# Cutting the first eight output tiles into smaller stores, and a later place for the scale and shift of two row groups

## Chip, cores, metric

One core of one Trainium2 chip (the other cores idle). The metric is the device time of one execution in microseconds.

## The reference, cut

Batch norm (training statistics, over the batch and the 16 x 16 block) of the outer products of all pairs of feature rows, then a multiplication by one 16 x 16 weight:

```python
# r_xi, r_xj: (1024, 39, 16); the 741 pairs are those with col < row
cross = xj[:, rows, :, None] * xi[:, cols, None, :]
mean = jnp.mean(cross, axis=(0, 2, 3), keepdims=True)
var = jnp.mean(jnp.square(cross - mean), axis=(0, 2, 3), keepdims=True)
normed = (cross - mean) * jax.lax.rsqrt(var + BN_EPS)
normed = normed * gamma[None, :, None, None] + beta[None, :, None, None]
out = normed[:, :, None, :, :] * W[None, None, :, :, :]     # 1024 x 1 x 741 x 16 x 16, f32
```

The inputs are 5 MB, the output 777 MB. Whatever else the kernel does, it has to write 777 MB.

## The kernel before

The batch lies on 128 partitions, 8 samples each. The statistics come first (to 37 us). Then the output is made tile by tile: a tile is one feature row `r` with its `r` pairs, for two samples of every partition. The tiles go in the order 19 (four tiles), then 20 and 18, 21 and 17, and so on to 38, so that the two tiles of every such couple have 38 pairs together. `y_sb` has room for two couples, so for four tiles: tile 12 goes where tile 8 and the first columns of tile 9 were. (In the profile DVE is VectorE, ACT is ScalarE, POOL is GpSimd and PE is TensorE; SP is SyncE, which issues the stores.)

Tiles 0 and 1 are made as raw products while the statistics run, and scaled, shifted and weighted when these are there. From tile 2 on, `xi` is scaled ahead (`scale_xi`, POOL), ACT and POOL make the products, and DVE adds the shift and multiplies by the weight in one instruction per pair (`finish`).

```python
ONE, TWO = 24, 31
FIRST_PIECES = ((0, 2, 8, 19), (0, 9, 19))
POOL_I, POOL_I_LONG = 4, 5
POOL_SHARE = 0.13
...
def products(n):
    xs = xs_of.pop(n)
    split = E - (POOL_I_LONG if tiles[n][0] > TWO else POOL_I)
    for t in range(T):
        for i in range(E):
            product(n, nc.scalar if i < split else nc.gpsimd, t, i, xs[:, t])

def store(n, c0, c1):                       # pairs c0 to c1 of tile n
    ...
    step = 1 if r > ONE and c1 == r else T
    for t in range(0, T, step):
        nc.sync.dma_start(out_v[...], view(n)[:, t : t + step, c0:c1, :]...)

def weigh(n, bounds):                       # tiles 0 and 1: times the weight, then store
    for c0, c1 in zip(bounds, bounds[1:]):
        nc.vector.tensor_tensor(y[:, :, c0:c1, :], y[:, :, c0:c1, :], w_dve..., ALU.mult)
        store(n, c0, c1)

def bounds(r):
    pieces = 1 + (r > ONE) + (r > TWO)
    return tuple(q * r // pieces for q in range(pieces + 1))

def finish(n):                              # tiles 2 and up
    split = r - int(r * POOL_SHARE + 0.5)
    ...                                     # POOL does pairs split to r
    for c0, c1 in zip(bounds(r), bounds(r)[1:]):
        for c in range(c0, min(c1, split)):
            stt(y[:, :, c, :], y[:, :, c, :], t_sb[...], w_dve..., ALU.add, ALU.mult)   # DVE
        store(n, c0, c1)
...
apply(0)                  # scale and shift of row 19, from PSUM into st_sb (DVE)
affine(0)                 # tile 0: scale and shift, ACT and POOL in turn
weigh(0, FIRST_PIECES[0])
scale_xi(2)
apply(1)                  # rows 15 to 18
apply(2)                  # rows 20 to 24
affine(1)
weigh(1, FIRST_PIECES[1])
for n in range(1, len(tiles)):
    if n == 1:
        products(2)
        scale_xi(3)
        continue
    if n + 2 < len(tiles):
        scale_xi(n + 2)
    finish(n)
    ...                   # apply of the later groups behind tiles 8, 16 and 24
    if n + 1 < len(tiles):
        products(n + 1)
```

## Time and profile before

| | before |
|---|---|
| median (lowest to highest) | 1895.81 us (1895.78 to 1895.99), 3 runs |
| span of the profiled execution | 1894.1 us |
| written | 776.99 MB |
| busy: DVE, ACT, POOL | 91%, 86%, 83% |
| DMA from 80 to 1850 us | share 0.98 to 1.04 in every stretch of 10 us and more |

A line of a view by stretches has the stretch and its length in us, the busy time and (in brackets) the instructions of PE, its weight load PEld, DVE, ACT and POOL, the granted clock, the DMA share (the mean busy share of the 16 DMA engines) and GB/s. A hole is a time in which the DMA moves nothing because no store is ready.

The chain that ended last, followed back from the end, in a stretch of the middle (start, length, what):

```profile
1418.35 4.62 DVE y_sb L233 x7
...
1423.03 13.14 DMA out_dram<-y_sb
...
1436.28 3.69 ACT y_sb L137 x6
...
1441.72 4.62 DVE y_sb L233 x7
```

A store lands, ACT may fill the place that has come free, DVE weights the products, the next store is issued and waits its turn in a full queue. A store's way from issue to landing (13.14 us) is over half of such a round (23 us from one DVE line to the next), and the DMA is busy throughout the round (share 1.00 from 1400 to 1600 us). Second, the instructions of ACT in the order of time around the first waits for a landed store (start, length, engine, line, operation, and in brackets the idle time before with what ended it):

```profile
170.63 1.51 ACT L137 ACTIVATE y_sb<-xs,xj_sb 128x336 f32<-128x336 f32 x3 [5.18 <-DMA out_dram<-y_sb]
```

At 170.63 us ACT has waited 5.18 us for tile 9 to land, whose place it needs for the second sample of tile 12. This moment will serve as a clock: it says when the stream of stores has got through tile 9, about 130 us after the first store.

### The profile page before, as it was taken

Reading aid. Unit: us, or ns where it says so; the run is one execution under the profiler, and the core shown is the slowest. Engines: PE = TensorE matmul, PEld = TensorE weight load, DVE = VectorE, ACT = ScalarE, POOL = GpSimd, SP = SyncE. Lnnn points to the kernel's source line nnn. Section 1 sums busy time; section 2 is a strip of 40 time slices with the busy share of each in tenths; the row PEclk is TensorE's granted clock in tenths of the full one; section 3 lists DMA queues with packets and bytes.
Section 4 is the critical chain, followed back from the end, with each engine's and each line's share of the span. In section 5 each row is a group of like instructions: output and inputs, shape, how many; then the busy total and the mean of one; then the engine's idle time right before and its main releaser. Section 6 shows DMA issues by size and latency. Waiting matters only on the chain. (4 is left out here: it accounts for less than half of the span.)

```text
span 1894.1 us, 10252 instructions
## 1 busy us (share of the span) xinstructions
PE 24.5 (1%) x128; PEld 23.1 (1%) x128; DVE 1730.9 (91%) x2609; ACT 1621.5 (86%) x3625; POOL 1574.5 (83%) x1985
## 2 busy tenths in 40 slices
PE   3100000000000000000000000000000000000000
PEld 3100000000000000000000000000000000000000
DVE  7999999998989898989898989899999999999996
ACT  8998989898989897989898989888888888888762
POOL 9797878787878787878787878898888888888972
DMA  3899999999999999999999999999999999999999
GB/s 147 362 426 430 425 430 426 427 428 422 430 424 425 424 425 425 424 426 424 423 426 424 425 424 422 424 421 421 421 421 421 418 414 420 414 418 417 417 418 389
DMA packets 67567, 783.67 MB, mean 414 GB/s; under 512 B 4896, under 2 KB 6048, under 8 KB 13728
## 3 DMA queue, kind: packets, MB, share of 16 engines
q1 hardware_dynamic: 66912, 780.46, 97.9%
q10 hardware_dynamic: 576, 2.56, 0.3%
q14 instruction: 78, 0.64, 0.1%
q8 instruction: 1, 0.02, 0.0%
HBM read 6.00 MB, written 776.99 MB: 413 GB/s over the span
## 5 line engine op out<-in xcount | busy, mean ns | idle before, releaser
L233 DVE SCALAR_TENSOR_TENSOR y_sb<-y_sb,st_sb,w_dve 128x512 f32<-128x512 f32 x2542 | 1678.7, 742 | 134.9 <-issue 133.0
L137 ACT ACTIVATE y_sb<-xs,xj_sb 128x256 f32<-128x256 f32 (+32 forms) x3544 | 1576.5, 537 | 228.4 <-DMA out_dram<-y_sb 170.3
L139 POOL TENSOR_SCALAR y_sb<-xs,xj_sb 128x560 f32<-128x560 f32 (+35 forms) x1256 | 643.0, 534 | 39.4 <-DMA out_dram<-y_sb 31.1
L225 POOL TENSOR_TENSOR y_sb<-y_sb,w_sb 128x1024 f32<-128x1024 f32 (+4 forms) x138 | 441.9, 3202 | 11.5
L157 POOL TENSOR_TENSOR xs<-xi_sb,st_sb 128x576 f32<-128x576 f32 (+37 forms) x150 | 187.8, 1252 | 225.9 <-ACT y_sb L137 213.8
L221 POOL TENSOR_SCALAR y_sb<-y_sb,st_sb 128x512 f32<-128x512 f32 x384 | 259.4, 691 | 13.1 <-ACT y_sb L137 13.1
L202 DVE TENSOR_TENSOR y_sb<-y_sb,w_dve 128x1024 f32<-128x1024 f32 (+4 forms) x5 | 20.9, 4205 | 3.9 <-ACT y_sb L192 3.9
L137 ACT ACTIVATE y_sb<-xi_sb,xj_sb 128x304 f32<-128x304 f32 x40 | 18.7, 534 | 0.1
L409 PE MATMUL ps<-y_sb 39*128 39x38 f32 (+37 forms) x76 | 16.5, 397 | 5.5 <-DVE y_sb L397 5.5
L409 PEld LDWEIGHTS ps<-y_sb 39*128 39x128 f32 x76 | 16.3, 329 | 5.7 <-issue 5.7
L192 ACT ACTIVATE y_sb<-y_sb,st_sb 128x512 f32<-128x512 f32 x20 | 14.2, 798 | 0.0
L194 POOL TENSOR_SCALAR y_sb<-y_sb,st_sb 128x512 f32<-128x512 f32 x18 | 13.5, 766 | 0.3 <-issue 0.3
L139 POOL TENSOR_SCALAR y_sb<-xi_sb,xj_sb 128x304 f32<-128x304 f32 x24 | 11.9, 528 | 0.0
L294 DVE TENSOR_REDUCE y_sb<-y_sb 128x78 f32<-128x1248 f32 x8 | 11.1, 1443 | 0.0
L288 ACT ACTIVATE y_sb<-y_sb 128x1248 f32<-128x1248 f32 x8 | 9.9, 1244 | 1.3 <-POOL y_sb L278 1.3
L272 DVE TENSOR_REDUCE y_sb<-xj_sb 128x78 f32<-128x1248 f32 (+1 forms) x5 | 5.9, 1189 | 5.5 <-DMA xj_sb<-in_r_xj_dram 5.5
L278 POOL TENSOR_TENSOR y_sb<-xj_sb,y_sb 128x1248 f32<-128x1248 f32 x4 | 9.3, 2322 | 1.9 <-ACT y_sb L322 1.9
L278 POOL TENSOR_TENSOR y_sb<-xi_sb,y_sb 128x1248 f32<-128x1248 f32 x4 | 9.3, 2329 | 0.0
L311 PE MATMUL ps<-y_sb 128*39 128x79 f32 x48 | 7.2, 339 | 16.6 <-DVE y_sb L294 16.6
L311 PEld LDWEIGHTS ps<-y_sb 128*39 128x39 f32 x48 | 6.1, 183 | 17.5 <-DVE y_sb L294 9.6
L272 DVE TENSOR_REDUCE y_sb<-xi_sb 128x78 f32<-128x1248 f32 (+1 forms) x5 | 5.9, 1186 | 0.1
L254 POOL TENSOR_SCALAR_AFFINE_SELECT y_sb<-y_sb 39x4992 f32<-39x4992 f32 x1 | 4.6, 4624 | 0.0
(45 smaller groups left out, 16.9 us busy)
## 6 DMA issues: line engine op xcount, KB each, us to landing
out_dram<-y_sb SPq DMA_DIRECT2D x32, 3072.0 KB, 13.7
out_dram<-y_sb SPq DMA_DIRECT2D x29, 2816.0 KB, 15.5
out_dram<-y_sb SPq DMA_DIRECT2D x32, 1664.0 KB, 14.3
out_dram<-y_sb SPq DMA_DIRECT2D x16, 3328.0 KB, 17.1
out_dram<-y_sb SPq DMA_DIRECT2D x12, 3840.0 KB, 17.6
out_dram<-y_sb SPq DMA_DIRECT2D x29, 1536.0 KB, 15.4
out_dram<-y_sb SPq DMA_DIRECT2D x12, 3584.0 KB, 18.4
out_dram<-y_sb SPq DMA_DIRECT2D x20, 1792.0 KB, 17.7
```

The source lines that it names most:

```text
L137: nc.scalar.activation(y, src, AF.Copy, scale=scale)
L139: engine.tensor_scalar(y, src, scale, 1.0, ALU.mult, ALU.mult)
L157: nc.gpsimd.tensor_tensor(xs, xi_sb[:, t0 : t0 + T, 0:r, :], s_sb[:, :, n0 : n0 + r, :].to_broadcast([P, T, r, E]), ALU.mult,)
L192: nc.scalar.activation(y[:, :, c, :], y[:, :, c, :], AF.Identity, bias=t_c, scale=s_c)
L194: nc.gpsimd.tensor_scalar(y[:, :, c, :], y[:, :, c, :], s_c, t_c, ALU.mult, ALU.add)
L202: nc.vector.tensor_tensor(y[:, :, c0:c1, :], y[:, :, c0:c1, :], w_dve.unsqueeze(1).to_broadcast([P, T, c1 - c0, EE]), ALU.mult,)
L221: nc.gpsimd.tensor_scalar(y[:, :, c, :], y[:, :, c, :], t_sb[:, n0 + c : n0 + c + 1], 1.0, ALU.add, ALU.mult)
L225: nc.gpsimd.tensor_tensor(y[:, :, split:r, :], y[:, :, split:r, :], w_sb.unsqueeze(1).to_broadcast([P, T, r - split, EE]), ALU.mult,)
L233: stt(y[:, :, c, :], y[:, :, c, :], t_sb[:, n0 + c : n0 + c + 1], w_dve.to_broadcast([P, T, EE]), ALU.add, ALU.mult,)
L278: nc.gpsimd.tensor_tensor(devs[n % 7], sources[x][:, t0 : t0 + T], shift[:, x : x + 1, :].unsqueeze(3).to_broadcast([P, T, F, E]), ALU.sub ...
L311: nc.tensor.matmul(acc[0:F, 0 : 2 * F + 1], lhs, fb[:, t], start=t == 0, stop=t == NT - 1)
L409: nc.tensor.matmul(ps[:, :, first[r] - n0 : first[r] - n0 + r], pick[:, r, :], stq[:, :, 0:r], start=True, stop=True,)
```

## The change

Intent: let the stream of stores run without holes in its first 40 us, by sending pieces as soon as they are weighted, and keep scale and shift of two row groups, which nobody needs yet, from standing ahead of tile 1. The core of the diff:

```diff
-FIRST_PIECES = ((0, 2, 8, 19), (0, 9, 19))
+FIRST_PIECES = (
+    (0, 2, 5, 9, 14, 19), (0, 6, 12, 19), (0, 4, 11, 19), (0, 9, 19), (0, 10, 20), (0, 9, 18), (0, 10, 20), (0, 9, 18)
+)
 ...
-    def bounds(r):
+    def bounds(n):
+        if n < len(FIRST_PIECES):
+            return FIRST_PIECES[n]
+        r = tiles[n][0]
         pieces = 1 + (r > ONE) + (r > TWO)
 ...
-        weigh(0, FIRST_PIECES[0])
+        weigh(0)
         scale_xi(2)
+        affine(1)
+        weigh(1)
+        apply(2)
         apply(1)
-        apply(2)
-        affine(1)
-        weigh(1, FIRST_PIECES[1])
```

(`weigh` and `finish` now ask `bounds(n)` instead of being given the bounds.)

More of the change, by code (lines that the diff above doesn't have):

```diff
@@ L196, in affine, with weigh @@
                 )
-    def weigh(n, bounds):
+    def weigh(n):
         y = view(n)
-        for c0, c1 in zip(bounds, bounds[1:]):
+        for c0, c1 in zip(bounds(n), bounds(n)[1:]):
             nc.vector.tensor_tensor(
@@ L230, in finish @@
             )
-        for c0, c1 in zip(bounds(r), bounds(r)[1:]):
+        for c0, c1 in zip(bounds(n), bounds(n)[1:]):
             for c in range(c0, min(c1, split)):
```

## The prediction

> **What bounds the kernel now.** I read four views in this order: the page's head, busy time by stretches, the instructions in order of time from 37 to 180 us, and the chain that ended last. The page first:
>
> ```profile
> PE 24.5 (1%) x128; PEld 23.1 (1%) x128; DVE 1730.9 (91%) x2609; ACT 1621.5 (86%) x3625; POOL 1574.5 (83%) x1985
> DMA  3899999999999999999999999999999999999999
> GB/s 147 362 426 430 425 430 426 427 428 422 430 424 425 424 425 425 424 426 424 423 426 424 425 424 422 424 421 421 421 421 421 418 414 420 414 418 417 417 418 389
> ```
>
> No compute engine is full, but the output (777 MB written) leaves at 414 to 430 GB/s from the third slice to the last but one, with the DMA digit at 9. So the end is set by when the stream of stores begins, by its holes, and by its rate. Holes show only in the first two slices (47 us each). Busy time by stretches there:
>
> ```profile
> 42.00:72.00 30.00, 11.19 (x52) 10.98 (x52) 28.90 (x23) 30.00 (x60) 23.80 (x34) 1.00 0.80 332
> 72.00:76.00 4.00, 0.00 (x0) 0.00 (x0) 4.00 (x7) 4.00 (x10) 2.45 (x4) 1.00 0.00 0
> 76.00:146.00 70.00, 0.00 (x0) 0.00 (x0) 69.97 (x109) 70.00 (x160) 64.61 (x84) 1.00 1.00 427
> ```
>
> Last two columns: DMA share and GB/s. From 42 to 72 us a fifth of the DMA time is empty, from 72 to 76 us all of it, after 76 us none. DVE is full in all three, so in this stretch DVE is what the DMA waits for. The instructions in order of time (start, length, engine) say why:
>
> ```profile
> 39.10 14.19 ACT L192 ACTIVATE y_sb<-y_sb,st_sb 128x512 f32<-128x512 f32 x20
> 40.00 1.22 DVE L202 TENSOR_TENSOR y_sb<-y_sb,w_dve 128x1024 f32<-128x1024 f32 x1 [2.14 <-ACT y_sb L192]
> 42.12 3.35 DVE L202 TENSOR_TENSOR y_sb<-y_sb,w_dve 128x3072 f32<-128x3072 f32 x1 [0.89 <-ACT y_sb L192]
> 46.35 6.02 DVE L202 TENSOR_TENSOR y_sb<-y_sb,w_dve 128x5632 f32<-128x5632 f32 x1 [0.88 <-ACT y_sb L192]
> ...
> 53.20 105.48 ACT L137 ACTIVATE y_sb<-xs,xj_sb 128x304 f32<-128x304 f32 x240
> ...
> 53.62 10.34 DVE L202 TENSOR_TENSOR y_sb<-y_sb,w_dve 128x4608 f32<-128x4608 f32 x2
> ...
> 63.94 77.11 DVE L233 SCALAR_TENSOR_TENSOR y_sb<-y_sb,st_sb,w_dve 128x512 f32<-128x512 f32 x117
> ...
> 159.75 5.70 ACT L137 ACTIVATE y_sb<-xs,xj_sb 128x336 f32<-128x336 f32 x12 [1.07 <-DMA out_dram<-y_sb]
> ```
>
> A store leaves only when its whole piece is weighted. A "pair" (one column of a tile, two rows of the batch) is 256 KiB, so at 427 GB/s it takes the DMA 0.614 us. DVE weights pairs of tiles 0 and 1 in 0.54 us each, of later tiles in 77.11/117 = 0.659 us, with 13% of them done on POOL. So DVE is a little faster than the DMA: tiles of 20 and 18 pairs cost it 33 x 0.659 = 21.7 us against 38 x 0.614 = 23.3 us of DMA. It fills the queue slowly, and only at 159.75 us does ACT first wait for a landed store. From there the chain of waits runs round as DMA, ACT, DVE, DMA, with the DMA never idle.
>
> **What the Trainium skill says.** "VectorE: DVE Perf Modes", section "The TRN2 errata", gives an fp32 tensor_tensor as (N+151)/0.96 ns. For 1024, 3072 and 5632 elements that is 1.22, 3.36 and 6.02 us; the trace has 1.22, 3.35 and 6.02. I use it for the new piece sizes. "DMA: Bandwidth & Descriptors", section "Anatomy of one DMA", has some 2.0 us fixed plus bytes/436e9 (fitted on the GpSimd path): for the first store of 512 KB 3.2 us, and the page shows 3.3 from issue to landing. Most of the fixed part is the landing's receipt, which a queue overlaps; what I charge a store that meets an idle queue is the start lag alone, about 0.85 us here (ready 75.15, bytes from 76.0). Section "Bandwidth" of that page measures 341 GB/s at 1 MB and 425 at 16 MB for single transfers; here queued stores of 1.5 to 6 MB reach 427, so pieces of 2.3 to 2.6 MB in a full queue should lose little.
>
> **The change part by part.**
>
> *Tile 0 in 2, 3, 4, 5, 5 pairs instead of 2, 6, 11.* Two more DVE instructions; the fixed 151 cycles (0.16 us) each, hidden since DVE waited 1.8 us on ACT here. ACT delivers every second pair each 0.71 us (14.19/20) from 39.9 us. First piece unchanged: ready 41.22. Then DVE, by the formula: 1536 elements from 41.42 to 43.2; 2048 to 45.4; 2560 to 48.2; 2560 to 50.9.
>
> *Tile 1 in 6, 6, 7, with scale and shift of two groups (1.3 us on DVE, from 52.28 to 53.62) moved behind it.* Pieces ready at 54.2, 57.5, 61.3 instead of 58.6 and 63.9; then the moved work to about 62.7. It is needed first by the scaling for tile 4 on POOL at 63.97 us, so it is in time by over 1 us. DVE does not start tile 2 earlier for it: tile 2 needs the last of 24 products on ACT, from 53.20 at 105.48/240 = 0.44 us each, done at 63.84. ACT's order is not changed. So tile 2 starts at 63.9 as before, and from there **DVE runs on the same clock as before**.
>
> *Tiles 2 to 7 in three or two pieces.* Same DVE instructions, stores earlier: tile 2 at 66.6, 71.2, 75.1 (before: 75.1); tile 3 at 81.1 and 86.3; and so on. Ten more stores in all, issued on SP, which does nothing else.
>
> *The DMA queue, worked out* (start = later of the end of the store ahead and ready + 0.85; 0.614 us a pair). Before: idle 10.5 us in sum (about 3 behind the first piece, 3 behind the second, 4.2 ahead of tile 2), then full from 76.0; tile 8 starts at 76.0 + 114 x 0.614 = 146.0. After: holes of some 0.6, 0.3 and 0.2 us in tile 0, 0.4 and 2.0 inside tile 2, 0.7 ahead of tile 3, 0.2 ahead of tile 4; the queue then ends tile 7 at about 140.4. Tile 8 (20 pairs, sent whole) is ready only after all 117 instructions, 63.94 + 77.11 = 141.05, so it starts at 141.9: **a new hole of 1.5 us**. Tiles 9, 10 and 11 (ready 152.3, 163.4, 174.0) are in time by about a microsecond or more, and DVE's lead grows again. Gain at tile 8: 146.0 - 141.9 = 4.1 us. From there on the DMA is full in both, so the gain goes to the end: 1895.8 - 4.1 = 1891.7.
>
> The gain is thus capped by DVE's pace to tile 8, not by the pieces: 1.5 us of loss in the pieces themselves would cost nothing.
>
> **The rivals.** *Given back later*: were the steady state set by something else than the stream of stores (the loop through ACT and DVE), the time would stay at 1895.8. Against it: DMA share 1.00 to 1.01 in every stretch from 76 to 1850 us; for it: the last 45 us, where DVE is busy 27.6 of 30 us and the DMA is at 0.96. *Small pieces slow the stream*: the late tiles, which leave in thirds, run at 414 to 421 GB/s against 428; 2% over the 75 us of tiles 2 to 7 is 1.5 us, just what the hole at tile 8 absorbs; beyond it the gain would be 3 us or less (1893). *More gain*: if the holes closed without the one at tile 8 (DVE a little faster, or the store starting sooner), up to 5.6 us: 1890.2. *DVE or POOL pushed back by the late scale and shift*: POOL's scaling for tile 4 would start after 64 us; it has an idle stretch of 1.6 us ahead of the next scaling, so one or two microseconds would vanish there.
>
> **Range and chances.** The cap (4.1) rests on measured durations and holds for small errors in the pieces; I put 1891.8, with 1890.2 (all holes closed) to 1893.8 (half the gain lost to slower stores or to the end). Two per cent is 38 us and all the idle time of the DMA before 76 us is some 10.5 behind the first store, so faster by 2% is out of reach, and nothing adds 38 us.
>
> **What the profile would show.** Right: DMA busy between 42 and 72 us at about 0.95 instead of 0.80; the empty stretch from 72 to 76 us gone; DVE's tile 2 still starting at 63.9; a hole of 1 to 2 us near 140.5 to 142 us; ACT's first wait for a store about 4 us earlier or shorter; the rate after 160 us unchanged. Wrong: a rate below 420 GB/s between 76 and 140 us; tile 2 starting after 64.5 us; new holes behind 160 us; a tail longer by what the start gained.

## The result, and the profile after

| | before | after |
|---|---|---|
| median of 6 runs | 1895.80 us | 1891.28 us |
| lowest to highest | 1895.55 to 1895.99 | 1891.05 to 1891.61 |
| span of the profiled execution | 1894.1 | 1889.3 |

The ratio is 0.9976 (95% interval 0.9963 to 0.9989). The gain is 4.5 us; 4.0 was predicted (4.1 in the working).

The page's slices of the kernel after:

```profile
DMA  4999999999999999999999999999999999999999
GB/s 164 390 418 429 425 427 429 430 424 429 424 425 426 424 424 426 422 425 425 424 425 423 426 423 426 422 422 422 421 421 422 418 415 419 416 419 419 415 419 390
```

The first two slices carry 164 and 390 GB/s instead of 147 and 362: the gain lies there. The third has 418 instead of 426, which was not in the working. Busy time by stretches, after (the last two columns are DMA share and GB/s):

```profile
42.00:72.00 30.00, 11.22 (x53) 11.01 (x52) 28.46 (x26) 30.00 (x60) 23.81 (x34) 1.00 0.91 367
72.00:76.00 4.00, 0.00 (x0) 0.00 (x0) 4.00 (x7) 4.00 (x10) 2.46 (x5) 1.00 0.98 401
76.00:136.00 60.00, 0.00 (x0) 0.00 (x0) 60.00 (x92) 60.00 (x138) 54.79 (x70) 1.00 1.00 417
...
140.00:142.00 2.00, 0.00 (x0) 0.00 (x0) 1.97 (x6) 2.00 (x5) 1.92 (x3) 1.00 0.75 313
...
70.00:72.00 2.00, 0.00 (x0) 0.00 (x0) 2.00 (x4) 2.00 (x6) 2.00 (x6) 1.00 0.16 64
80.00:82.00 2.00, 0.00 (x0) 0.00 (x0) 2.00 (x4) 2.00 (x6) 2.00 (x5) 1.00 0.80 332
```

The empty stretch from 72 to 76 us is gone. What is left of holes is where the working has them: inside tile 2 (70 to 72 us, share 0.16), ahead of tile 3 (80 to 82), and ahead of tile 8 (140 to 142, share 0.75, so half a microsecond). The instructions of DVE and ACT in the order of time, after:

```profile
63.96 77.11 DVE L238 SCALAR_TENSOR_TENSOR y_sb<-y_sb,st_sb,w_dve 128x512 f32<-128x512 f32 x117 [1.44 <-ACT y_sb L139]
140.99 0.26 DVE L425 TENSOR_TENSOR ps<-ps,st_sb 128x105 f32<-128x105 f32 x1
```

```profile
166.31 6.11 ACT L139 ACTIVATE y_sb<-xs,xj_sb 128x336 f32<-128x336 f32 x13 [2.02 <-DMA out_dram<-y_sb]
```

DVE starts tile 2 at 63.96 us (before: 63.94), and is through tile 8 at 141.0 (before: the same): its clock has not moved, although it now stands idle for 1.44 us ahead of tile 2, waiting for ACT. And the clock of the stream, the landing of tile 9, is at 166.31 instead of 170.63 us: 4.3 us earlier. Of the gain at the end, 4.3 of 4.5 us are there within the first 170 us; from 200 us to 1800 the rates of the two kernels are alike within 2 to 3 GB/s in every 100 us.

### The profile page after: what moved, and what is told of

It is laid out like the page before. It is cut to its first block, busy times and chain, and to the rows that moved or that the text cites. A ratio compares the mean times of both kernels' runs of the same rounds, so it can differ in the third digit from the quotient of the medians.

```text
span 1889.3 us, 10288 instructions
## 1 busy us (share of the span) xinstructions
PE 24.5 (1%) x128; PEld 23.1 (1%) x128; DVE 1730.7 (92%) x2612; ACT 1621.3 (86%) x3625; POOL 1574.5 (83%) x1985
## 5 line engine op out<-in xcount | busy, mean ns | idle before, releaser
L204 DVE TENSOR_TENSOR y_sb<-y_sb,w_dve 128x2560 f32<-128x2560 f32 (+5 forms) x8 | 21.0, 2682 | 2.3 <-ACT y_sb L194 2.3
L141 POOL TENSOR_SCALAR y_sb<-xi_sb,xj_sb 128x304 f32<-128x304 f32 x24 | 11.9, 518 | 0.0
```

What stands on the lines that cost most here:

```text
L141: engine.tensor_scalar(y, src, scale, 1.0, ALU.mult, ALU.mult)
```

## The experiments

Twelve kernels were run, all with correct results. They came in four groups; each kernel ran five rounds, or three where noted, and beside the kernel before on the same chip.

| run | what it is | median us | ratio to before | 95% interval |
|---|---|---|---|---|
| order_only | old pieces, new order | 1895.69 | 0.9999 | 0.9987 to 1.0012 |
| pieces_only | new pieces, old order | 1891.11 | 0.9976 | 0.9963 to 0.9990 |
| tiles01 | new pieces in tiles 0 and 1 alone | 1895.87 | 1.0000 | 0.9987 to 1.0012 |
| tiles27 | new pieces in tiles 2 to 7 alone | 1893.20 | 0.9986 | 0.9974 to 0.9999 |
| tiles03 | new pieces in tiles 0 to 3 | 1894.18 | 0.9992 | 0.9979 to 1.0006 |
| no_pool (3 rounds) | DVE does POOL's pairs in tiles 2 to 7 | 1900.19 | 1.0024 | 1.0011 to 1.0038 |
| all_half (3 rounds) | tiles 8 to 43 in two pieces too | 1897.17 | 1.0009 | 0.9995 to 1.0022 |
| late_two | over 31 pairs: two pieces for three (and, by mistake, less for POOL) | 1889.58 | 0.9968 | 0.9955 to 0.9980 |
| pool6 | POOL makes more of tile 2's products | 1889.46 | 0.9967 | 0.9954 to 0.9981 |
| late_two_b | over 31 pairs: two pieces for three | 1886.50 | 0.9952 | 0.9939 to 0.9964 |
| combo | pool6 and late_two_b | 1885.03 | 0.9944 | 0.9932 to 0.9957 |
| combo_whole | combo, 25 to 31 pairs in one piece | 1896.90 | 1.0007 | 0.9994 to 1.0021 |

The intervals are a quarter of a per cent wide, some 5 us, and by themselves they can't part effects of one or two. But the runs of one kernel lie within 0.2 to 0.8 us of each other, and the kernel before has medians of 1895.56 to 1895.80 us in all groups. Differences under half a microsecond are not interpreted below. All edits are to the changed kernel. It was not run again beside them: gains over it are taken from its 1891.28 us above, across chips on which the kernel before differs by up to 0.24 us.

### Which part carries the gain: order_only and pieces_only

```diff
+FIRST_PIECES = ((0, 2, 8, 19), (0, 9, 19))                # order_only: the rest as changed
```
```diff
         weigh(0)                                          # pieces_only: the old order
         scale_xi(2)
+        apply(1)
+        apply(2)
         affine(1)
         weigh(1)
-        apply(2)
-        apply(1)
```

> The changed kernel with the old pieces (tile 0 in 2, 6, 11 pairs, tile 1 in 9, 10, the rest whole), so that only scale and shift stand behind tile 1. My theory: tile 1's pieces are ready 1.3 us earlier but stand behind tile 0's last piece in the queue (which ends near 60 us), the hole ahead of tile 2 stays, gain 0.0 us: 1895.8. Rival (the order is a part of the gain): 1894.5, 1.3 us less than before.

> The changed kernel with the old order (scale and shift of the two groups between tile 0 and tile 1), all new pieces kept. My theory: a hole of about 1 us appears ahead of tile 1's first piece, but tile 2's second piece still waits for DVE at 71.2 us and tile 8 for DVE at 141.05 us, so the end does not move: 1891.3. Rival (order matters by its 1.3 us): 1892.6.

Measured: 1895.69 us (before 1895.70) and 1891.11 us. The later place of scale and shift is worth nothing, alone or with the pieces. In order_only the stretch ahead of tile 2 is as empty as before (busy time by stretches, order_only):

```profile
72.00:76.00 4.00, 0.00 (x0) 0.00 (x0) 4.00 (x7) 4.00 (x10) 2.49 (x5) 1.00 0.01 3
```

What moved earlier on DVE stood behind other bytes in the queue, and tile 2 waits for ACT's products and not for DVE. In pieces_only a hole comes earlier (DMA share 0.93 instead of 0.97 from 42 to 64 us) and the one inside tile 2 shrinks by as much (0.51 instead of 0.16 from 70 to 72 us); from 42 to 72 us both kernels write 367 GB/s.

### Early holes or all tiles: tiles01, tiles03, tiles27

```diff
+FIRST_PIECES = ((0, 2, 5, 9, 14, 19), (0, 6, 12, 19))                                   # tiles01
+FIRST_PIECES = ((0, 2, 5, 9, 14, 19), (0, 6, 12, 19), (0, 4, 11, 19), (0, 9, 19))        # tiles03
+FIRST_PIECES = ((0, 2, 8, 19), (0, 9, 19), (0, 4, 11, 19), (0, 9, 19), (0, 10, 20), ...)  # tiles27
```

> New pieces for tiles 0 and 1 alone, tiles 2 to 7 whole. My theory: the holes between 42 and 60 us are closed, but tile 2 is ready whole at 75.1 us as before, the empty stretch ahead of it grows to about 8 us, gain 0: 1895.8. Rival (the holes filled up to 60 us, some 6 us, are what pays): 1890 to 1892.

> New pieces for tiles 0 to 3, tiles 4 to 7 whole. My theory: tile 3 ends near 94 us on the DMA, but tile 4 is ready whole only at 97.55 us and starts at 98.4, against 76.0 + 38 x 0.614 = 99.3 before: gain 0.9 us, 1894.9. Rival (the early holes alone pay): 1891.3.

> New pieces for tiles 2 to 7 alone, tiles 0 and 1 in the old pieces. My theory: the queue is full from 53 us on, tile 1 ends near 71.7 us, tiles 2 to 7 (114 pairs) at the 417 GB/s measured with such pieces take 71.7 us, tile 8 starts near 143.4 us instead of 146.0 (before) and 142 (change): gain 2.5 us, 1893.3. Rival (DVE's pace at tile 8 is the only limit): 1891.3; rival (all of the gain is in tile 0): 1895.8.

Measured: 1895.87, 1894.18 and 1893.20 us, so gains of -0.2, 1.4 and 2.5 us (0, 0.9 and 2.5 expected). The reason is in the stretches of the three traces, tiles01, tiles03 and tiles27 in this order:

```profile
42.00:72.00 30.00, 11.10 (x52) 10.89 (x52) 28.45 (x26) 30.00 (x59) 23.79 (x34) 1.00 0.83 332
72.00:76.00 4.00, 0.00 (x0) 0.00 (x0) 4.00 (x7) 4.00 (x10) 2.46 (x4) 1.00 0.00 0
```
```profile
94.00:98.00 4.00, 0.00 (x0) 0.00 (x0) 4.00 (x7) 4.00 (x10) 3.92 (x8) 1.00 0.00 0
```
```profile
42.00:72.00 30.00, 11.20 (x52) 10.99 (x52) 28.90 (x23) 30.00 (x60) 23.81 (x34) 1.00 0.81 333
72.00:76.00 4.00, 0.00 (x0) 0.00 (x0) 4.00 (x7) 4.00 (x10) 2.46 (x4) 1.00 1.03 413
76.00:136.00 60.00, 0.00 (x0) 0.00 (x0) 60.00 (x92) 60.00 (x138) 54.81 (x70) 1.00 1.01 421
```

In tiles01, up to 72 us the DMA moves exactly what it moved before (332 GB/s on the mean): the smaller pieces close holes early in the stretch, and the same time is lost at its end, since tile 2 is ready at 75.1 us whatever happens ahead of it. In tiles03 the empty stretch has moved on to 94 to 98 us, ahead of tile 4, the first whole one. Only where the pieces reach on does the gain stay. Tiles27 in turn keeps the early holes and has a queue that never runs dry behind 53 us; it gains 2.5 us. The parts don't add: 0 for tiles 0 and 1, 2.5 for tiles 2 to 7, 4.5 for both. A hole closed early is worth something only if the stores behind it can use the room.

In tiles03 ACT's wait for tile 9 ends at 169.66 us, 0.97 us earlier than before, as expected (0.9); the other half microsecond at the end comes later and is not explained.

### Is DVE's pace the cap: no_pool and pool6

```diff
-        split = r - int(r * POOL_SHARE + 0.5)                        # no_pool, in finish
+        split = r - int(r * POOL_SHARE + 0.5) if n > 7 else r
```
```diff
-        split = E - (POOL_I_LONG if tiles[n][0] > TWO else POOL_I)   # pool6, in products
+        split = E - (6 if n == 2 else POOL_I_LONG if tiles[n][0] > TWO else POOL_I)
```

> The changed kernel, but in tiles 2 to 7 DVE takes POOL's 14 pairs as well (14 x 0.659 = 9.2 us more on DVE before tile 8). My theory (DVE's pace to tile 8 caps the start of the full stream): tile 8 ready at 150.3 instead of 141.05 us, starts 9.2 us later, and the end moves by the same: 1900.5. Rival (DVE is off the path once stores leave in pieces; the stream's bytes set the end): 1891.3.

> The changed kernel with POOL taking 6 instead of 4 of the 16 products of each row in tile 2 alone (POOL stands idle for 6.1 us there, DVE waits 1.44 us for ACT's last product). My theory (the end is set by when DVE gets through to tile 8): ACT ends tile 2's products 4 x 0.44 = 1.8 us earlier, DVE starts tile 2 at once behind scale and shift, at 62.5 instead of 63.96 us, tile 8 is ready 1.4 us earlier and the end comes 1.4 us earlier: 1889.8. Rival (the cap at tile 8 is by now the bytes of the stream, whose pieces cost it time): at most 0.5 us: 1890.8 or more.

Measured: 1900.19 us, 8.9 later than the changed kernel (9.2 expected), and 1889.46 us, 1.8 earlier (1.4 expected). The instructions of DVE in the order of time, first no_pool, then pool6; and one stretch of no_pool:

```profile
63.65 86.33 DVE L238 SCALAR_TENSOR_TENSOR y_sb<-y_sb,st_sb,w_dve 128x512 f32<-128x512 f32 x131 [1.45 <-ACT y_sb L139]
149.90 0.27 DVE L425 TENSOR_TENSOR ps<-ps,st_sb 128x105 f32<-128x105 f32 x1
```
```profile
62.27 77.11 DVE L238 SCALAR_TENSOR_TENSOR y_sb<-y_sb,st_sb,w_dve 128x512 f32<-128x512 f32 x117
139.29 0.27 DVE L425 TENSOR_TENSOR ps<-ps,st_sb 128x105 f32<-128x105 f32 x1
```
```profile
145.00:150.00 5.00, 0.00 (x0) 0.00 (x0) 5.00 (x9) 5.00 (x12) 3.71 (x6) 1.00 0.07 28
```

In no_pool DVE is through tile 8 at 149.9 instead of 141.0 us, 8.9 later; ahead of it the DMA stands still (share 0.07); the end is 8.9 later. In pool6 it is through at 139.3, 1.7 earlier; the end is 1.8 earlier. So the end follows the moment at which DVE is through tile 8, in both directions, and both rivals are out as they were put. No_pool is the sharper test: there the hole inside tile 2 is as before (share 0.13 from 70 to 72 us). Pool6 moved DVE's whole clock, and so closed most of that hole too; a smaller one stays ahead of tile 8 (pool6):

```profile
70.00:72.00 2.00, 0.00 (x0) 0.00 (x0) 2.00 (x4) 2.00 (x6) 1.10 (x3) 1.00 0.83 340
139.00:141.00 2.00, 0.00 (x0) 0.00 (x0) 1.97 (x6) 2.00 (x5) 2.00 (x1) 1.00 0.80 334
```

So pool6 alone does not tell the cap at tile 8 from the hole inside tile 2 with the bytes behind it. In the changed kernel these two limits lie half a microsecond apart (the hole left ahead of tile 8): by that estimate a DVE that were faster between tiles 3 and 8 alone would gain no more than this; it was not run.

### What a piece costs the stream: all_half

```diff
-        pieces = 1 + (r > ONE) + (r > TWO)
+        pieces = 1 + (n < 44) + (r > ONE and n >= 44) + (r > TWO)
```

> The changed kernel with tiles 8 to 43 in two pieces each as well (36 more stores, 9216 more rows). My theory: each row of a store costs the stream a fixed time, by the rates of 417 and 427 GB/s with and without pieces about 0.28 us for 256 rows: 36 x 0.28 = 10 us longer, 1901.4, and 417 GB/s between 200 and 440 us. Rival (a full queue hides the row's fixed time; the 417 came from holes): 1891.3 and 428 GB/s.

Measured: 1897.17 us, 5.9 longer than the changed kernel, not 10. The stretch from 200 to 440 us, first of the changed kernel, then of all_half:

```profile
200.00:440.00 240.00, 0.00 (x0) 0.00 (x0) 228.55 (x351) 218.71 (x497) 203.49 (x263) 1.00 1.01 428
```
```profile
200.00:440.00 240.00, 0.00 (x0) 0.00 (x0) 225.47 (x346) 212.57 (x482) 196.46 (x253) 1.00 1.01 421
```

The DMA is full in both, and the same bytes in twice as many rows of half the length (7 to 12 KB instead of 14 to 24) go at 421 instead of 428 GB/s. So the effect is there, and a full queue doesn't hide it; its size is 5.9/36 = 0.16 us per added store of 256 rows. Whether the store or its rows cost the time, no run separates, since every piece that was added or dropped here is 256 rows for one store. A hint for the rows: from 566 to 840 us of the changed kernel two neighbours take 4 stores, as many as in all_half above, but 768 rows instead of 1024, and the rate there is 425 GB/s. My 0.28 came from 417 against 427 GB/s, and the 417 had the hole ahead of tile 3 in it: tiles27, with no hole in the same stretch, has 421 as well.

### The other way: late_two, late_two_b, combo, combo_whole

If every row costs the stream, fewer pieces late should pay.

```diff
-ONE, TWO = 24, 31                                # late_two
+ONE, TWO = 24, 38
```
```diff
-        pieces = 1 + (r > ONE) + (r > TWO)
+        pieces = 1 + (r > ONE)                   # late_two_b, and combo with pool6's line
+        pieces = 1 + (r > TWO)                   # combo_whole, with pool6's line
```

> The changed kernel with the tiles of more than 31 pairs in two pieces instead of three (28 tiles, 7168 rows fewer). My theory: 28 x 0.28 = 7.8 us shorter if the queue stays full, 1883.5, and 420 GB/s or more instead of 416 between 1500 and 1800 us. Rival (the larger pieces leave and land later, ACT and DVE wait longer for places, and holes open in the stream): 1891 or more.

> late_two made clean: there the limit that was changed also took one product in 16 from POOL and gave it to ACT in the tiles over 31 pairs, by my mistake; here only the pieces go from three to two. By the stores of all_half, 256 rows cost 5.9/36 = 0.16 us, so 28 x 0.16 = 4.6 us shorter if the queue stays full: 1886.7. Rival (larger pieces leave later and open holes, whoever makes the products): near late_two's gain of 1.7 us: 1889.6.

> pool6 and late_two_b together. My theory: the first moves the start of the full stream, the second its rate, so the gains add: 1891.3 - 1.8 - 4.8 = 1884.7. Rival (the two share a limit): 1886 or more.

> combo with the tiles of 25 to 31 pairs sent in one piece of rows (28 tiles, 7168 rows fewer again; still two stores, one for each row of the batch). My theory of the row cost: 28 x 0.16 = 4.6 us less, 1880.1, and 425 to 428 GB/s instead of 422 between 1100 and 1500 us. Rival (a whole tile of 25 and more pairs leaves and lands so late that ACT waits for places and holes open): 1884.7 or more.

Late_two gained 1.7 us over the changed kernel where I expected 7.8. It was not clean: `TWO` also decides in which tiles POOL makes 5 instead of 4 of 16 products, so ACT had more to do in the tiles over 31 pairs. Late_two_b changes the pieces alone: 1886.50 us, 4.8 less than the changed kernel, as all_half's 0.16 us per store of 256 rows says (4.6). The stretches 1500 to 1800 and 1800 to 1850 us of the changed kernel, of late_two and of late_two_b:

```profile
1500.00:1800.00 300.00, 0.00 (x0) 0.00 (x0) 274.33 (x416) 244.00 (x544) 263.32 (x323) 1.00 1.00 416
1800.00:1850.00 50.00, 0.00 (x0) 0.00 (x0) 45.78 (x70) 32.51 (x48) 35.22 (x34) 1.00 0.99 417
```
```profile
1500.00:1800.00 300.00, 0.00 (x0) 0.00 (x0) 275.30 (x417) 264.90 (x575) 243.08 (x297) 1.00 0.99 418
1800.00:1850.00 50.00, 0.00 (x0) 0.00 (x0) 44.34 (x68) 34.03 (x49) 32.82 (x30) 1.00 0.97 411
```
```profile
1500.00:1800.00 300.00, 0.00 (x0) 0.00 (x0) 275.95 (x418) 248.82 (x550) 262.58 (x324) 1.00 1.00 420
1800.00:1850.00 50.00, 0.00 (x0) 0.00 (x0) 45.67 (x70) 30.69 (x44) 37.13 (x39) 1.00 1.00 424
```

My reading is that larger pieces leave less time between a piece's landing and the next need of its place. Where ACT is loaded more (265 us busy of 300 instead of 249), the share falls to 0.97 at the end; with POOL's share kept, the DMA is full at 420 and 424 GB/s.

Combo is the best version found: 1885.03 us, ratio 0.9944 to before, 6.3 us less than the changed kernel by the medians (1.8 + 4.8 = 6.6 expected).

Combo_whole goes too far: 1896.90 us, 11.9 worse than combo. The stretches 1000 to 1100 and 1100 to 1200 us, combo, then combo_whole:

```profile
1000.00:1100.00 100.00, 0.00 (x0) 0.00 (x0) 92.25 (x141) 89.58 (x201) 82.95 (x111) 1.00 1.01 424
1100.00:1200.00 100.00, 0.00 (x0) 0.00 (x0) 92.17 (x140) 87.53 (x198) 81.97 (x107) 1.00 1.01 424
```
```profile
1000.00:1100.00 100.00, 0.00 (x0) 0.00 (x0) 87.53 (x133) 84.72 (x192) 78.42 (x103) 1.00 0.95 404
1100.00:1200.00 100.00, 0.00 (x0) 0.00 (x0) 87.06 (x133) 84.74 (x192) 77.83 (x101) 1.00 0.94 400
```

In this stretch, where tiles of 29 to 31 pairs leave whole, 5 to 6% of the DMA's time is empty. From 600 to 800 us (25 to 27 pairs) the share is 0.99 to 1.00 and the rate 421 to 426, about that of combo; a limit in between was not tried.

## Why the prediction was right, step by step

- **The bound.** Right. The output leaves at the same rate in both kernels behind 200 us, and what is gained by 170 us (4.3 us) is there at the end (4.5).
- **The pieces and their times on DVE.** Right: tile 2 starts at 63.96 us in spite of an earlier end of tile 1, waiting 1.44 us for ACT; DVE is through tile 8 at 141.0 us as before.
- **The order.** Right that it does not let tile 2 start earlier. The prediction gave it no share of its own; order_only and pieces_only show none.
- **The cap at tile 8.** Right, and the main term: no_pool and pool6 move the end by what they move DVE's passage through tile 8 (+8.9 for +8.9 us, -1.8 for -1.7). 4.1 us were worked out there, 4.3 measured at tile 9's landing.
- **The hole of 1.5 us ahead of tile 8.** Mis-sized: about 0.5 us (share 0.75 in 140 to 142 us). The term that failed is "pieces of 2.3 to 2.6 MB in a full queue should lose little". They run at 421 instead of 428 GB/s; tiles 2 to 7 have seven stores more, and 7 x 0.16 = 1.1 us fills most of the hole. As the prediction said of its cap, that costs nothing at the end: tile 8 starts when DVE lets it. But only 0.5 of the 1.5 us that it called free were left, and its own rival put the loss of the pieces at all of the 1.5: that the number held is in part luck. The reading behind the term, that stores of 1.5 to 6 MB reach 427, was wrong: those from 76 to 146 us have 4608 to 5120 KB, and the kernel before already held the rate for smaller ones in a full queue, where the two pieces of tile 1 (2304 and 2560 KB) leave:

```profile
60.00:70.00 10.00, 0.00 (x0) 0.00 (x0) 10.00 (x11) 10.00 (x24) 5.95 (x7) 1.00 1.00 416
```

- **What would show it wrong.** The prediction named "a rate below 420 GB/s between 76 and 140 us". That was met (417), and the time was right all the same: the test was badly chosen, as the text ahead of it had already argued that the hole at tile 8 absorbs such a loss. Of its signs of being right, "DMA busy between 42 and 72 us at about 0.95" does not follow from its own list, which has 3.5 us of holes in these 30 and so leaves 0.88; measured 0.91. The hole of 1 to 2 us near 140.5 us is about 0.5. "DMA share 1.00 to 1.01 in every stretch" was read too closely: it is 0.98 to 1.04 in stretches of 10 us, and 0.99 from 1800 to 1850 us.
- **The rival of small pieces that slow the stream.** True in mechanism, and without effect here. Tiles27, where the queue stays full up to tile 8, comes out 1.9 us behind the full change; its early holes and the slower pieces are both in that, and in it the bytes of the small pieces, not DVE, decide when tile 8 starts (share 0.96 to 1.08 in every microsecond from 138 to 143 us, so no hole).

Left open: the last 0.2 us of the change's gain and 0.5 us in tiles03, which come behind 170 us; and whether it is the store or its rows that cost time.

## What to carry to other kernels

In a kernel bound by its output stream, a hole early in the stream is worth closing only as far as the producer can keep the queue filled from there on; work out the queue store by store (ready time, bytes, the end of the one ahead) up to the place where the producer's lead is large enough. Then cut small only as far as that place, and as coarse as the buffers allow behind it, since here every added store of 256 rows cost a full queue 0.16 us, and too coarse opened holes. And when a constant is changed for an experiment, look where else it is read.

## What the Trainium skill lacked or had wrong

- "DMA: Bandwidth & Descriptors", section "Bandwidth": it has sizes of single transfers (341 GB/s at 1 MB, 425 at 16 MB) and speaks of small descriptors up to some hundred bytes. It has nothing on long rows in a full queue. Here stores in rows of 7 to 12 KB instead of 14 to 24 KB ran at 421 instead of 428 GB/s with the DMA share at 1.01 in both; 36 more stores of 256 rows took 5.9 us, 28 fewer saved 4.8.
- The same page, "Where 436 GB/s comes from", says that for transfers between HBM and SBUF the HBM side (about 358 GB/s) binds. One core alone wrote 428 GB/s over 240 us; "HBM Reference", section "Specifications (TRN2)", has the right sentence for it (about 425 for a core streaming alone).
- The same page, "Anatomy of one DMA", puts most of the fixed 2 us at the landing, for the GpSimd path; no page splits it for a store from the sync engine. Here the sum fits (3.3 us for the first store of 512 KB, 3.2 by the formula), but about half of the fixed part comes first: issued at 41.25 us, its bytes flow from about 42.2 to 43.6, and it lands near 44.5. "Latency and other measured facts" of that page has about 0.6 us for the first byte.
- No page says how large a store may grow before holes open in the stream: in combo_whole the share fell to 0.94 with whole tiles of 29 to 31 pairs, where two pieces kept it at 1.01.
